# Two attention layers on one core: scores turned round, with queries on partitions and keys along the free axis

## The chip, the core and the metric

The kernel runs on one core of a Trainium2 chip. The core has a matrix engine (TensorE, PE in the profile), a vector engine (VectorE, DVE), an activation engine (ScalarE, ACT), GpSimd (POOL) and a queue engine (SP) that here issues transfers between the device memory and the core's SBUF. Matrix products land in PSUM, in banks of 512 fp32 values on each of 128 partitions. The metric is the device time of one execution in microseconds; lower is better.

## The reference, cut to what matters

Four batch elements (B = 4) with 256 queries of width 512 pass two blocks, each a cross-attention over the same 1601 context rows and a linear layer, with a layernorm in front and the input added behind. All is fp32.

```python
# layer 0: 16 heads; queries and keys of a head are 32 wide, the keys are shared by all heads
C_q, C_kv = Q @ Wq_d, K @ Wkv_d                      # 64 and 32 wide
q = (C_q @ W_qk).reshape(b, n, 16, 32)
attn = softmax(einsum('bnhl,bkl->bhnk', q, C_kv) / sqrt(32))
V = (C_kv @ Wv_u).reshape(b, nkv, 16, 32)
x = x + einsum('bhnk,bkhd->bnhd', attn, V).reshape(b, n, 512)
x = x + layernorm(x) @ dequantize_int4(W0).T + bias
# layer 1: 16 query heads of width 96 on 4 key and value heads; hidden = context and the 256 latents
q, k, v = latents @ Wq.T, hidden @ Wk.T, hidden @ Wv.T     # 1857 keys
x = x + (softmax(q k / sqrt(96)) v) @ Wo.T
H = layernorm(x) @ W1.T + b1
x = x + H + gated low-rank term                       # a few per cent of the work
```

## The kernel before

**Order.** The kernel is written as tasks (`Plan.task`), each with an engine, an estimated duration, its dependencies and the buffers it makes or uses. `Plan.order` runs a list schedule over them with these estimates, nine rounds, and the best round gives the order in which each engine's instructions are written out. On the chip every engine works through its own list in that order; an instruction that waits holds what stands behind it on its engine. `STAGE` and `LINE` fix which heads come next: first the 16 layer 0 heads of batch element 0, then three mixed stages with the 16 layer 1 heads of one element between the 16 layer 0 heads of the next, then the last 16 layer 1 heads. A change of the tensor engine's tile shape is estimated at 0.2 us (`SWITCH`), and a task of another shape is held back a little (`HOLD`).

**A head** (`Head.schedule`). Scores stand with keys on partitions and the 256 queries along the free axis: one 128-key tile gives 128 x 256. In `Head0.score_units` (L1628) and `Head1.score_units` (L1779) four key tiles are computed at a time in four 32-row tiles of the array; a layer 1 head, 96 deep, takes three such steps for each tile, accumulated. Queries are replicated to the four row groups through device memory (`l0_query`, `l0_query_pair`, L787; `l1_query`, L1025 to L1028 and `to_groups`, L362). The score tiles lie in PSUM in two buffers of two banks (`s_psum`). Then, for each head:
- ScalarE copies the scores to SBUF (L1480), four key tiles at a time;
- VectorE takes the maximum over key tiles (L1498, L1501, L1506); TensorE transposes it (L1529), VectorE reduces over the keys that now lie along the free axis (L1533), and TensorE spreads the result back over all partitions (L1542): one maximum for each query;
- VectorE subtracts it (L1554), ScalarE takes the exponential in place (L1563).

**Products.** In layer 1 (`Head1.product_units`, L1804) the stationary operand is a 128-key tile of the values with a column of ones (97 columns), the moving one the 128 x 256 weights: 15 products for each head, and the last row of the result is the softmax's denominator. In layer 0 three tiles and a tile of ones go side by side in column tiles of 32 (`units_of_three`, L1726), with sums on VectorE (`add_up`, L1668, L1671); the first batch element takes two column tiles of 64 (`units_of_two`, L1700). Layer 1 divides after the products (`l1_normalise`), layer 0 in `l0_output`.

**Around the heads.** Keys (`keys`, L923), values (`values`, L863), queries (L1013), output products (`l1_output`, L1161), the linear layers (`linear`, L636) and the latents of the context (`l0_latents`, L663) are full 128 x 128 products over four chunks of the input width, one PSUM bank each (`aux_psum`, two buffers), and are planned into the gaps between heads. The context of one batch element, 3.3 MB, is loaded once into one buffer (`load_ctx`, from ScalarE's queue); keys stay in SBUF in four row groups, values in two halves.

```python
def score_units(self):                                # Head1, before
    def unit(slot, c, step, pss):
        for r in range(4):
            if 4 * slot + r < NK1:
                part = slice(r * 32, (r + 1) * 32)
                nc.tensor.matmul(
                    pss[2 * step + r // 2][:, 2 * (r % 2) + slot % 2, :],
                    lhsT=s["kT", self.kv].tile[part, c, slot, :],
                    rhs=s["q1", self.kv][self.g].tile[part, c, :], ...)
```

Of the kernel before, what the change touches and what calls it, by code (L numbers as in the profile page):

```python
# [14 lines left out]
P = 128  # L15
# [46 lines left out]
class Plan:  # L62
# [11 lines left out]
    def task(self, eng, us, what, deps=(), prio=0.0, new=(), uses=(), lag=0.0, form="full"):  # L74


        t = Task(eng, us, what, [d for d in deps if d is not None], round(prio, 4), new, len(self.tasks))
        t.lag, t.form = lag, form
        for b in (*new, *uses):
            b.users.append(t)  # L80
        self.tasks.append(t)
        return t

    def forward(self, busy):
# [26 lines left out]
        while len(done) < len(self.tasks):  # L111
            best = None
            for eng, tasks in ready.items():
                for t in tasks:
# [6 lines left out]
                    stays = eng != "PE" or t.form == form  # L121
# [12 lines left out]
            t.start = key[0]  # L134
            if t.eng == "PE" and t.form != form:
                t.start += self.SWITCH
            free[t.eng] = t.start + t.us
            if t.eng == "PE":
                form = t.form
            t.end = t.start + t.us + t.lag  # L140
# [15 lines left out]
    def backward(self, done):  # L156
# [13 lines left out]
        for _ in range(len(done)):  # L170
# [8 lines left out]
            free[t.eng] = key[0] + t.us  # L179
# [10 lines left out]
    def order(self, busy):  # L190
        for t in self.tasks:
            for d in t.deps:
                d.next.append(t)
        best = None
        for i in range(self.ROUNDS + 1):
            done = self.forward(busy)
            end = max(t.end for t in done)
            if best is None or end < best[0]:
                best = (end, done)
            self.backward(done)  # L200
        return best[1]
# [3 lines left out]
def xattn_ffn_x2_kernel(  # L205
# [37 lines left out]
    def s_psum(name):  # L243
        return psum.tile([P, 4, T], F32, tag="s", bufs=2, name=name)

    def m_psum(name):
        return psum.tile([P, 2, T], F32, tag="m", bufs=1, name=name)

    def o_psum(name):
        return psum.tile([P, 2, T], F32, tag="o", bufs=1, name=name)  # L250

    def aux_psum(name):
        return psum.tile([P, 512], F32, tag="aux", bufs=2, name=name)
# [4 lines left out]
    DUP = (FULL + 1) * P - S  # L258


# [18 lines left out]
    nc.vector.tensor_scalar(ident, count, number, None, ALU.is_equal)  # L279
    wq_d_sb = const.tile([P, NC, LQ], F32, name="wq_d_sb")  # L280
# [10 lines left out]
    BLOCKS = [(0, 512), (512, 512), (1024, S - 1024)]  # L291

    def load_ctx(b, queue=nc.scalar, between=lambda: None):
        t = big.tile([P, NC, S], F32, tag="ctxT", name=f"ctxT_{b}")
        src = ctxT[b].rearrange("(c p) s -> p c s", p=P)
        for a, w in BLOCKS:
            queue.dma_start(out=t[:, :, a : a + w], in_=src[:, :, a : a + w])
            if a == 0:
                between()
# [3 lines left out]
    KV_ORDER = [3, 0, 1, 2]  # L303
    wvT_sb = const.tile([P, NC, KV * HD], F32, name="wvT_sb")

    def load_wv():
        src = wvT.rearrange("(c p) n -> p c n", p=P)
        nc.sync.dma_start(out=wvT_sb[:, :, :HD], in_=src[:, :, 3 * HD :])
        nc.sync.dma_start(out=wvT_sb[:, :, HD:], in_=src[:, :, : 3 * HD])

    first_ctx = load_ctx(0, nc.sync, load_wv)


    WV = (((0, 64), (32, 96)), ((0, 32, 64), (96,)))
    wv_h = [const.tile([P, H0, 33], F32, name=f"wv_{len(rows)}") for rows, _ in WV]

# [6 lines left out]
    for c in range(NC):  # L323
        src = wkT[c * P : (c + 1) * P, :]
        nc.sync.dma_start(
            out=wk_sb[:, c, :, 0:HD],
            in_=src[:, : 3 * HD].rearrange("p (i d) -> p i d", i=3),
        )
        nc.sync.dma_start(
            out=wk_sb[:, c, :, HD:P],  # L330
            in_=src[:, 3 * HD :].rearrange("p (i d) -> p i d", i=3),
        )
# [10 lines left out]
    ctx_at = [t * P for t in range(FULL)] + [S - P]  # L343
    NK0 = FULL + 1
    NK1 = NK0 + NQ
    VW = HD + 1

    ORDER0 = [[0, 4, 1, 5], [2, 6, 3, 7], [8, 12, 9], [10, 11]]  # L350
    ORDER1 = [[0, 4, 1, 5], [2, 6, 3, 7], [8, 12, 9, 13], [10, 14, 11]]

    G_ORDER = [0, 1, 2, 3]

    rsums = tc.dram_tile([B * KV, G * T], F32, name="rsums")
    q0_rows = [tc.dram_tile([P, 2 * T], F32, name=f"q0_rows_{i}") for i in range(2 * B)]

    q_rows = [tc.dram_tile([32, 3 * T], F32, name=f"q_rows_{i}") for i in range(B * KV * G)]

    def to_groups(dst, far):  # L360
        for r in range(4):
            nc.sync.dma_start(  # L362
                out=dst[32 * r : 32 * r + 32].rearrange("l c t -> l (c t)"), in_=far
            )

# [4 lines left out]
    def late_constants():  # L370
        def values(w, rows, picks):
            def blank():
                nc.gpsimd.memset(w, 0.0)
                for r in picks:
                    nc.gpsimd.memset(w[r : r + 1, :, 32:33], 1.0)

            def load():
                for r in rows:
                    nc.sync.dma_start(
                        out=w[r : r + L0, :, 0:32], in_=wv_u.rearrange("l (h d) -> l h d", d=32)  # L380
                    )

            t = task("POOL", 0.9, blank, [], 0.0)
            return task("SP", 0.45 * len(rows), load, [t], 0.0, lag=2.5)
# [11 lines left out]
        book["wv"] = [values(w, *at) for w, at in zip(wv_h, WV)]  # L396
        t = task("POOL", 0.2, clear, [], 12.0)
        book["limes"] = task("SP", 3.6, experts, [t], 12.0, lag=2.5)

# [12 lines left out]
    def item(name, steps, evictions, deps, prio, uses=(), new=(), form="full"):  # L412
# [3 lines left out]
        ps = Buf("aux", 2)  # L416
        last = None
        for us, what in steps:
# [58 lines left out]
    def layernorm(b, name, tag, prio):  # L477
# [65 lines left out]
        for q in range(NQ):  # L543
# [19 lines left out]
                [(xnT, [P, NC, T])] if first else (),  # L563
            )
# [67 lines left out]
    def linear(b, name, xnT, deps, w, prio):  # L632
        for q in range(NQ):

            def step(ps, c, q=q):
                nc.tensor.matmul(  # L636
# [15 lines left out]
    def l0_latents(b, deps, prio):  # L652

        cT = st8[b]["cT"]
        ckvT, ckv = Buf("ckvT", 1), Buf("ckv", 1)


        def step(ps, s):
            for c in range(NC):
                for r in range(4):  # L660
                    t = 4 * s + r
                    if t < NK0:
                        nc.tensor.matmul(  # L663
                            ps[r * L0 : (r + 1) * L0, s * P : (s + 1) * P],
                            lhsT=wkv_d_sb[:, c, :],
                            rhs=cT.tile[:, c, ctx_at[t] : ctx_at[t] + P],
                            start=(c == 0),
                            stop=(c == NC - 1),
                        )

        def clear():
            ckvT.tile = work.tile([P, 4, P], F32, tag="ckvT", bufs=1, name=f"ckvT_{b}")
            nc.gpsimd.memset(ckvT.tile[:, 3, :], 0.0)

        def keep(ps):
            flat = ckvT.tile.rearrange("p s k -> p (s k)")
            nc.scalar.copy(flat[:, : 3 * P], ps[:, : 3 * P])
            nc.scalar.copy(flat[0:L0, 3 * P :], ps[0:L0, 3 * P :])

        t = task("POOL", 0.2, clear, [], prio, [ckvT])  # L680
        done = item(
            f"ckv_ps_{b}",
            chain(4, 1.0, step),
            [("ACT", 0.75, keep, [ckvT], [t])],
            [*deps, t],
            prio,
            [cT],
            form="32 columns",
        )

        def transpose(ps, s):
            nc.tensor.transpose(ps[:, s * P : (s + 1) * P], ckvT.tile[:, s, :], ident)

        def values(ps):
            nc.scalar.copy(
                ckv.tile[:, :, 0, :], ps[:, : NK0 * L0].rearrange("p (t l) -> p t l", l=L0)
            )

        def mask():
            nc.gpsimd.memset(ckv.tile[0:DUP, FULL, :, :], 0.0)  # L700


        def ones():
            ckv.tile = work.tile([P, NK0, 2, L0], F32, tag="ckv", bufs=1, name=f"ckv_{b}")
            nc.gpsimd.memset(ckv.tile[:, :, 1, :], 1.0)

        t = task("POOL", 0.5, ones, [], prio, [ckv])
        turned = item(
            f"ckv_tp_{b}",
            chain(4, 0.11, transpose),  # L710
            [("ACT", 0.59, values, [ckv], [t])],
            [*done, t],
            prio,
            [ckvT],
        )
        st8[b]["ckvT"], st8[b]["ckv"] = ckvT, ckv
        st8[b]["ckvT_done"] = done
        st8[b]["ckv_done"] = [task("POOL", 0.2, mask, turned, prio, uses=[ckv])]

    def l0_query_latent(b, xnT, deps, prio):  # L720
        cqT = Buf("cqT", 1)

        def step(ps, c):
            nc.tensor.matmul(
# [7 lines left out]
        def keep(ps):  # L732
# [11 lines left out]
            "64 columns",  # L744
        )

    def l0_query(b, half, prio):

        stage, cqT, far = Buf("q0s", 1), st8[b]["cqT"], q0_rows[2 * b + half]

        def step(ps, i):
            quad = 2 * half + i
            nc.tensor.matmul(
                ps[:, i * T : (i + 1) * T],
                lhsT=w_qk_sb[:, quad * P : (quad + 1) * P],
                rhs=cqT.tile,
                start=True,
                stop=True,
            )

        def keep(ps):
            nc.scalar.copy(stage.tile, ps)

        def away():
            nc.sync.dma_start(out=far, in_=stage.tile)

        t = item(
            f"q0_ps_{b}_{half}",
            chain(2, mm(T), step),
# [1327 lines left out]
```

## Time and profile before

| | us |
|---|---|
| median of three timed runs (lowest, highest) | 1906.34 (1903.82, 1907.99) |
| profiled execution, first to last instruction (span) | 1899.4 |
| TensorE busy in it | 1844.9 |
| VectorE busy | 1434.3 |
| ScalarE busy | 1149.0 |
| GpSimd busy | 111.7 |

The profile is of one execution, and gives no time for it but its span; the timed runs lie some 7 us above that. "Busy" adds up the instructions that the profiler recorded, with each instant given to one group of instructions. An fp32 matrix product leaves two records on PE, and a transpose one; PEld are the weight loads, which mostly run under earlier products. A row of the groups names the line, engine, operation, result and operands with their shapes, the count, then busy time and the mean of one, then the idle time of the engine ahead of it and what ended that.

### The profile page before, as it was taken

Reading aid. Unit: us, or ns where it says so; the run is one execution under the profiler, and the core shown is the slowest. Engines: PE = TensorE matmul, PEld = TensorE weight load, DVE = VectorE, ACT = ScalarE, POOL = GpSimd, SP = SyncE. Lnnn points to the kernel's source line nnn. Section 1 sums busy time; section 2 is a strip of 40 time slices with the busy share of each in tenths; the row PEclk is TensorE's granted clock in tenths of the full one; section 3 lists DMA queues with packets and bytes.
Section 4 is the critical chain, followed back from the end, with each engine's and each line's share of the span. In section 5 each row is a group of like instructions: output and inputs, shape, how many; then the busy total and the mean of one; then the engine's idle time right before and its main releaser. Section 6 shows DMA issues by size and latency. Waiting matters only on the chain.

```text
span 1899.4 us, 37000 instructions
## 1 busy us (share of the span) xinstructions
PE 1844.9 (97%) x15223; PEld 1295.7 (68%) x15223; DVE 1434.3 (76%) x2200; ACT 1149.0 (60%) x1695; POOL 111.7 (6%) x185
## 2 busy tenths in 40 slices
PE   6999999999999999999999999999999999999996
PEld 4665787676766777666676677766767667777773
DVE  2998358999998554899999835699999964367773
ACT  2888356677676533767677633566767754365550
POOL 1110100000000110000000101000000010100000
PEclk8999999999999999999999999999999999999998
DMA  7210131311100234121100143222110015111121
GB/s 212 66 42 12 66 83 46 83 49 32 37 18 12 66 103 145 46 65 39 38 24 9 23 107 99 96 65 67 32 32 15 10 45 131 54 40 37 40 71 60
DMA packets 116721, 110.03 MB, mean 58 GB/s; under 512 B 69005, under 2 KB 85353, under 8 KB 116169
## 3 DMA queue, kind: packets, MB, share of 16 engines
q1 hardware_dynamic: 110232, 96.98, 18.4%
q10 hardware_dynamic: 6320, 10.69, 1.7%
q8 instruction: 120, 1.97, 0.4%
q14 instruction: 49, 0.39, 0.1%
HBM read 94.46 MB, written 13.17 MB: 57 GB/s over the span
## 4 chain that ended last, share of the span: by engine, by line
PE 83%; DVE 7%; issue 3%; DMA 3%; ACT 2%; SPq 1%; POOL 0%; DVEq 0%; ACTq 0%; POOLq 0%
PE o L1804 20%; PE s L1779 16%; PE v_ps L863 7%; PE k_ps_c L923 6%; PE s L1628 6%; PE o L1726 5%; PE q_ps L1013 4%; PE wo_ps L1161 4%; PE f L636 3%; DVE mx L1501 3%; PE o L1700 2%; DVE S L1554 2%; PE pm L1529 2%; PE pm L1542 2%; PE vu_ps L804 1%
## 5 line engine op out<-in xcount | busy, mean ns | idle before, releaser
L1480 ACT COPY S<-s 128x1024 f32<-128x1024 f32 (+2 forms) x512 | 448.6, 906 | 332.7 <-PE s L1779 121.6
L1554 DVE TENSOR_TENSOR S<-S,pm 128x1024 f32<-128x1024 f32 (+2 forms) x512 | 528.8, 1082 | 36.5 <-PE pm L1542 34.5
L1501 DVE TENSOR_TENSOR mx<-mx,S 128x512 f32<-128x512 f32 (+1 forms) x704 | 463.7, 659 | 116.9 <-ACT S L1480 92.1
L1563 ACT ACTIVATE S<-S 128x1024 f32<-128x1024 f32 (+2 forms) x512 | 472.3, 950 | 124.4 <-DVE S L1554 118.4
L1804 PE MATMUL o<-S,v 128*97 128x256 f32 x1920 | 461.7, 382 | 3.8 <-ACT S L1563 2.5
L1804 PEld LDWEIGHTS o<-S,v 128*97 128x97 f32 x1920 | 301.6, 164 | 113.7 <-issue 24.7
L1779 PE MATMUL s<-q,kT_k_ps_c 32*128 32x256 f32 x4320 | 275.9, 383 | 0.0
L1779 PEld LDWEIGHTS s<-q,kT_k_ps_c 32*128 32x128 f32 x4320 | 225.0, 185 | 48.8 <-issue 20.8
L863 PE MATMUL v_ps<-wvT_sb,ctxT 128*128 128x192 f32 x832 | 158.9, 334 | 11.8 <-DMA wvT_sb<-in_wvT 11.7
L923 PE MATMUL k_ps_c<-ctxT,wk_sb 128*128 128x384 f32 (+1 forms) x480 | 157.9, 455 | 0.9 <-DVE xnT_xn_tp_a L541 0.9
L863 PEld LDWEIGHTS v_ps<-wvT_sb,ctxT 128*128 128x128 f32 x832 | 136.0, 192 | 32.0 <-issue 16.4
L1628 PE MATMUL s<-q,ckvT 32*128 32x256 f32 x1664 | 150.9, 411 | 5.2 <-DMA q<-q_rows 4.8
L1628 PEld LDWEIGHTS s<-q,ckvT 32*128 32x128 f32 x1664 | 93.5, 185 | 57.0 <-issue 27.0
L1726 PE MATMUL o<-S,ckv 128*32 128x256 f32 x1728 | 127.4, 384 | 0.6 <-DVE S L1671 0.4
L1498 DVE TENSOR_TENSOR mx<-S 128x512 f32<-128x512 f32 x128 | 89.0, 695 | 46.1 <-ACT S L1480 45.5
L923 PEld LDWEIGHTS k_ps_c<-ctxT,wk_sb 128*128 128x128 f32 x480 | 78.7, 189 | 45.4 <-issue 15.5
L1013 PE MATMUL q_ps<-xnT_xn_tp_a,wq 128*128 128x256 f32 x384 | 98.3, 387 | 0.9 <-ACT p_q_ps L1022 0.9
L1533 DVE TENSOR_REDUCE m<-pm 128x2 f32<-128x256 f32 x128 | 53.9, 421 | 56.3 <-PE pm L1529 55.7
L933 ACT COPY kT_k_ps_c<-k_ps_c 32x384 f32<-32x384 f32 (+1 forms) x180 | 76.8, 427 | 32.2 <-PE k_ps_c L923 30.0
L1671 DVE TENSOR_TENSOR S<-S,S 128x512 f32<-128x512 f32 x144 | 88.3, 613 | 9.9 <-ACT S L1480 0.5
L1779 PE MATMUL s<-q,kTlast_k_ps_c 32*128 32x256 f32 x1440 | 93.7, 385 | 0.0
L1161 PE MATMUL wo_ps<-wo,oT 128*128 128x512 f32 x192 | 92.3, 604 | 0.0
(143 smaller groups left out, 1427.8 us busy)
## 6 DMA issues: line engine op xcount, KB each, us to landing
q<-q_rows SPq DMA_DIRECT2D x256, 96.0 KB
wq<-in_wqT SPq DMA_DIRECT2D x48, 192.0 KB
wo<-in_woT SPq DMA_DIRECT2D x16, 576.0 KB
q<-q_rows SPq DMA_DIRECT2D x128, 64.0 KB
ctxT<-in_ctxT ACTq DMA_DIRECT2D x6, 1024.0 KB
q_rows<-p_q_ps SPq DMA_DIRECT2D x48, 96.0 KB
rb<-rsums SPq DMA_DIRECT2D x15, 288.0 KB
ctxT<-in_ctxT ACTq DMA_DIRECT2D x3, 1154.0 KB
```

The lines of the kernel that those rows point to most:

```text
L863: nc.tensor.matmul(ps[:, i * 2 * HD : (i + 1) * 2 * HD], lhsT=src.tile[:, c, tiles[i][1] : tiles[i][1] + P], rhs=wvT_sb[:, c, half * 2 * H ...
L923: nc.tensor.matmul(out, lhsT=wk_sb[:, c, i, :], rhs=rhs, start=(c == 0), stop=(c == NC - 1),)
L1013: nc.tensor.matmul(ps[:, :T], lhsT=wq.tile[:, c, :], rhs=xnT.tile[:, c, :], start=(c == 0), stop=(c == NC - 1),)
L1161: nc.tensor.matmul(ps, lhsT=oT.tile[:, i, q * P : (q + 1) * P], rhs=wo.tile[:, i, :], start=(i == 0), stop=(i == G - 2),)
L1480: nc.scalar.copy(S4[g].tile[:, :n, :], self.scored(ps[g].tile, g))
L1501: nc.vector.tensor_tensor(mx.tile[:, :w, :], mx.tile[:, :w, :], t[:, a : a + w, :], ALU.max)
L1554: nc.vector.tensor_tensor(s[:, :n, :], s[:, :n, :], om.tile[:, 1:2, :].to_broadcast([P, n, T]), ALU.subtract,)
L1563: nc.scalar.activation(s[:, :n, :], s[:, :n, :], AF.Exp, scale=self.scale)
L1628: nc.tensor.matmul(pss[2 * step + r // 2][:, 2 * (r % 2) + s % 2, :], lhsT=st8[self.b]["ckvT"].tile[part, s, :], rhs=qr[part, self.h % 2, ...
L1726: nc.tensor.matmul(po[32 * r : 32 * r + 32, :], lhsT=lhsT, rhs=rhs, start=start, stop=stop)
L1779: nc.tensor.matmul(pss[2 * step + r // 2][:, 2 * (r % 2) + slot % 2, :], lhsT=s["kT", self.kv].tile[part, c, slot, :], rhs=s["q1", self.kv ...
L1804: nc.tensor.matmul(po[:VW, :], lhsT=s["v", j // 2].tile[:, t, j % 2, :], rhs=self.S[g].tile[:, i, :], start=(k == 0), stop=(k == NK1 - 1),)
```

## The change

Scores are turned round: queries on partitions, keys along the free axis. With that the maximum of a query lies within a partition, and the weights have to be turned before the product with the values.

- **Scores.** A unit of layer 1 takes 32 queries of a head as the stationary operand, in each of the four column tiles of the array, and 480 keys as the moving one: column tile c holds the keys whose place in their 128-key tile is 32c to 32c+31. The 96 dimensions are one step. In layer 0 (K = 32) a unit is 16 tiles of 32 x 32: four row groups with four query blocks, into four banks, by four column tiles. Scores lie in a ring of six PSUM banks (`banks`); missing keys are columns filled once with a large negative number.
- **Softmax.** VectorE reduces each bank along the free axis, straight from PSUM. The four column tiles hold four parts of one query's keys, so their maxima meet in a small product (`gather`) with a constant matrix `place`, followed by a small minimum (the sign and the scale are in `place`). ScalarE takes the exponential from PSUM with that as its bias, and sums it (`accum_out`) in the same instruction. VectorE turns the result in 32 x 32 blocks into `Pt`, keys on partitions. The copy to SBUF, the full transposes, the subtraction and the sums of `add_up` are gone. Layer 1 does this for two banks at a time, layer 0 for four.
- **Products.** Four column tiles with the values as the stationary operand: layer 1 packs the 12 blocks of 32 value columns of a group's four heads into three units, layer 0 two heads with two key tiles each. The denominators come from the exponentials' sums.
- **Dense products** go through a helper, `matmul`, that splits the stationary operand into four column tiles of 32; most of the work then has one tile shape. Layernorm's transposes stay full. `aux_psum` has one buffer (`NA = 1`).
- **Transfers.** The replication of the queries is gone. Keys and values pass through device memory (`k_rows`, `v_rows`), where the parts of a group are put together, and come back for each key head (`load_keys`, `load_values`). The context comes in blocks of 384 keys (the last 449) in two buffers, blocks 0 and 1 twice (`SWEEP`), from SP's queue. `STAGE` is a new pattern, "1111" + "0001010101" * 2 + "00101011".

```diff
-    def s_psum(name):
-        return psum.tile([P, 4, T], F32, tag="s", bufs=2, name=name)
+    NB, NA = 6, 1
+    banks = psum.tile([P, NB, 512], F32, tag="s", bufs=1, name="banks")
...
+    def matmul(out, lhsT, rhs, start, stop):
+        for a, w in splits(lhsT.shape[-1], 32):
+            nc.tensor.matmul(
+                out[a : a + w], lhsT=lhsT[:, a : a + w], rhs=rhs, start=start, stop=stop
+            )
...
+            def peaks(j, step):
...
+                nc.vector.tensor_reduce(
+                    mx.tile[:, k : k + step],
+                    banks[:, ps[j].at : ps[j].at + step, self.skip :],
+                    AX.X,
+                    ALU.max,
+                )
...
+            def gather():
+                for c in range(4):
+                    nc.tensor.matmul(
+                        banks[32 * c : 32 * c + 32, ps[blocks[0]].at, : 4 * w],
+                        lhsT=place[:, self.layer, :],
+                        rhs=mx.tile[:, lo:hi],
...
+                nc.scalar.activation(
+                    ex[j // 2].tile[:, j % 2, :n],
+                    banks[:, ps[j].at, self.skip :],
+                    AF.Exp,
+                    bias=mx.tile[:, k : k + 1],
+                    scale=SCALES[self.layer],
+                    accum_out=self.sum_at(4 * m + j),
+                )
...
+                nc.vector.transpose(
+                    self.Pt.tile[:, : n // 32, 32 * j : 32 * j + 64].rearrange(
+                        "p b (j i) -> p j b i", i=32
+                    ),
+                    ex[k].tile[:, :, :n].rearrange("p j (b i) -> p j b i", i=32),
+                )
...
+            def unit():                                     # Head0
+                for r in range(4):
+                    for c in range(4):
+                        n, part = N0 + SHORT[c], slice(32 * r, 32 * r + 32)
+                        nc.tensor.matmul(
+                            banks[32 * c : 32 * c + 32, ps[r].at, self.skip : self.skip + n],
+                            lhsT=s["q0", self.h // 8].tile[part, self.h % 8, 32 * m : 32 * m + 32],
+                            rhs=s["ckvT"].tile[part, c, :n],
...
+            def unit(j):                                    # Head1
+                q = 32 * (4 * m + j)
+                for c in range(4):
+                    n = N1 + SHORT[c]
+                    nc.tensor.matmul(
+                        banks[32 * c : 32 * c + 32, ps[j].at, self.skip : self.skip + n],
+                        lhsT=s["q1", self.kv].tile[:, self.g, q : q + 32],
+                        rhs=s["kT", self.kv].tile[:, c, :n],
...
+            blocks = [divmod(4 * p + j, 3) for j in range(4)]
+
+            def unit(t, po):
+                for j, (h, c) in enumerate(blocks):
+                    nc.tensor.matmul(
+                        po[32 * j : 32 * j + 32, :],
+                        lhsT=v.tile[:, t, 32 * c : 32 * c + 32],
+                        rhs=heads[h].Pt.tile[:, t, :],
...
```

Here N0 is 416 and N1 480, `skip` the rest of a bank's 512 columns, `w` the number of banks treated together, `m` the half of a head's eight blocks of 32 queries.

## The prediction

> **What bounds the kernel now.** I read the page's first two parts, then busy time by stage (cut where the first feed-forward product of each batch element ends), then the groups by line. Engine, busy microseconds, share and instructions:
>
> ```profile
> PE 1844.9 (97%) x15223; PEld 1295.7 (68%) x15223; DVE 1434.3 (76%) x2200; ACT 1149.0 (60%) x1695; POOL 111.7 (6%) x185
> PE   6999999999999999999999999999999999999996
> PEclk8999999999999999999999999999999999999998
> ```
>
> TensorE is the bound from the second slice to the last but one, at full clock. By stage (length, then PE, weight loads, VectorE and ScalarE busy):
>
> ```profile
> 0.00:228.00 228.00, 207.70 (x1463) 136.07 (x1464) 153.99 (x249) 146.78 (x230) 27.53 (x52) 0.98 0.25 72
> 228.00:641.60 413.60, 407.32 (x3619) 284.60 (x3618) 352.09 (x537) 278.34 (x403) 17.53 (x32) 1.00 0.18 49
> 641.60:1099.50 457.90, 452.07 (x3830) 316.72 (x3829) 364.89 (x557) 286.24 (x421) 24.69 (x39) 1.00 0.20 57
> 1099.50:1557.70 458.20, 453.26 (x3840) 318.01 (x3840) 365.05 (x558) 286.85 (x423) 23.98 (x37) 1.00 0.20 57
> 1557.70:1899.40 341.70, 324.52 (x2480) 240.32 (x2478) 198.33 (x301) 150.79 (x218) 18.00 (x25) 0.98 0.23 63
> ```
>
> VectorE stands at 80% in the mixed stages: not much of TensorE's time can go before VectorE is next. Prices of matmuls come from the chain of waits, where runs without a gap stand (start, length, records):
>
> ```profile
> 247.19 2.80 PE s L1779 x48
> 1633.49 9.10 PE v_ps L863 x56
> 1642.59 3.45 PE o L1804 x16
> ```
>
> L1804 takes 0.216 us a record of 256 columns, L863 0.163 us for 192: 0.84 ns a column. Every fp32 product leaves two records, so a matmul of 256 columns costs 0.432 us. L1779, four row tiles at once, takes 2.80 us for 48 records, six units of four: 0.43 us a unit and 0.2 for the start. The timeline shows the same of four column tiles (L1726, 24 records = three units), with the shapes beside it:
>
> ```profile
> 423.16 2.12 PE L863 MATMUL v_ps<-wvT_sb,ctxT 128*128 128x192 f32 x12
> 425.21 1.50 PE L1726 MATMUL o<-S,ckv 128*32 128x256 f32 x24
> 426.64 0.43 PE L1542 MATMUL pm<-ident,m 128*128 128x128 f32 x2
> ```
>
> So four packed tiles cost what one full matmul of the same columns costs, and a change of shape costs extra: 12 x 0.163 us from 423.16 ends at 425.11, the next shape starts at 425.21. Over the trace's 746 changes of shape the wait has a median of 0.094 us, and the first pass, with weights not loaded ahead, is about 0.07 late: 0.165 a change.
>
> With these prices (transposes leave one record, 0.107 us) PE's order gives 190, 395, 440, 440 and 312 us for the stages, changes included: 1776 in all. The stages are 38, 19, 18, 18 and 30 us longer: the start (PE waits 11.7 us for its first weights), short waits, the tail. The sum describes this kernel to within those 123 us; I use it for the new one.
>
> **The change, TensorE.** Counts are from PE's instruction order, whole kernel:
> - Layer 1 scores: 768 units of 256 columns (331.6 us) become 512 of 480 (0.805 each, 412.2): +80.6. Here it loses: 96 of 128 rows are used, before all were.
> - Layer 1 products: 960 of 256 (414.4) become 720 packed units (310.8): -103.6. Twelve 32-wide value blocks of four heads fill three units, and the row of ones goes.
> - Layer 0 scores: 256 units (110.5) become 128 units of 16 tiles and 416 columns (0.698 each, 89.4): -21.1.
> - Layer 0 products: 352 units (151.9) become 224 (96.7): -55.2.
> - Keys, values, output projections of layer 0: -11; the dense products split into four column tiles keep their columns.
> - The transposes around the maximum, 512 records, 55 us, go; 384 gathers of four small matmuls come. Their nearest row is L663, the same packed shape with 128 columns: 3.61 us for 16 units in the chain, 0.23 each, 88 us: +33. Bounds: 0.11 (stream alone) and 0.30 (L1206, 4.8 us for 16 matmuls of 8 columns).
> - Changes of shape: 746 become 341: -67.
>
> Sum -142. By stage the new order needs 162, 375, 407, 406 and 283 us.
>
> **The change, VectorE.** Priced from these groups (count, busy, mean ns):
>
> ```profile
> L1554 DVE TENSOR_TENSOR S<-S,pm 128x1024 f32<-128x1024 f32 (+2 forms) x512 | 528.8, 1082 | 36.5 <-PE pm L1542 34.5
> L1501 DVE TENSOR_TENSOR mx<-mx,S 128x512 f32<-128x512 f32 (+1 forms) x704 | 463.7, 659 | 116.9 <-ACT S L1480 92.1
> L1533 DVE TENSOR_REDUCE m<-pm 128x2 f32<-128x256 f32 x128 | 53.9, 421 | 56.3 <-PE pm L1529 55.7
> L1480 ACT COPY S<-s 128x1024 f32<-128x1024 f32 (+2 forms) x512 | 448.6, 906 | 332.7 <-PE s L1779 121.6
> ```
>
> Subtractions, maxima and sums (some 1300 us) go. In come 512 reductions of 480 and 256 of 832 from PSUM (0.66 and 1.03 us: L1533's 0.421 at 256, with the 1.06 ns a column between L1501's 256 and 512 forms), 602 us; 768 tiny operations (0.19, as L1287 at 32 columns), 146 us; and 512 block transposes of 960 or 832 columns. No row shows these. Below, the cast (0.45 us for 512) gives 0.85; above, the slowest row by column is the reciprocal (1.75 us for 256), 6.5 us. I take the elementwise rows, which also read and write SBUF once: 1.18 and 1.05, 571 us. With the 135 of the rest: about 1450, as before; a mixed stage gets 360 of its 430 us.
>
> The Trainium skill, "VectorE: DVE Perf Modes", section "The three transpose paths", has 311 ns for a 128x128 block transpose in bf16. Scaled in proportion, an estimate, that is 2.3 us for 960 columns, and VectorE would reach 2000 us; with its fixed part paid once it is 1.2. No row here decides.
>
> **ScalarE** loses its copies (448.6 us); the exponentials read PSUM, 0.56 and 0.51 us by L1480's slope, plus a bias and a running sum that no row shows: 0 to 0.26 us more (the shortest copy). 715 to 980 us, off the path except through the banks.
>
> **Queues.** SP loses 384 query loads and 104 query stores, and gets 168 key stores, 60 value stores, 64 reads back and 24 context blocks; it issues 609 transfers, was 772. A store waits on SP for ScalarE's eviction, and the query weights' loads stand behind it; they are two buffers deep, so I set that at nothing (uncovered: the eviction, 0.5 us, for each of 57 a stage, at most 30 us). DMA engines were 18% busy. The key and value round trip takes the place of the query round trip ahead of each layer 1 (4.1 us there); I set it at no cost, covered by the leftover context products; uncovered, 5 us a stage.
>
> **What is new on the path: the first stage.** Layer 0's unit takes four of six PSUM banks, so the next waits for two exponentials of the one before: scores 0.9 with their drain, two reductions 2.1, tiny operation 0.2, gather 0.4, tiny 0.2, two exponentials 1.3, handoffs 0.4: 5.5 to 5.9. Thirty-two of these, 25 us ahead and 12 behind: 225 us, where TensorE needs 162 (plus 12 of start). This stage gains 3, not 28. Elsewhere the gather adds a queue: PE runs its planned order, so a gather that waits for VectorE holds every product behind it; on ScalarE the exponentials wait for the gather's result, and the evictions of the dense products stand behind them. There are 96 in a mixed stage against 64 pairs of transposes, so I raise the 18 us of waits to 25; the tail keeps 30.
>
> Sum: 225 + 400 + 432 + 431 + 313 = 1801 against 1899.4. The median of the timed runs, 1906.3, lies 7 us above the profiled span: about 1808, -5%.
>
> **Rivals.**
> 1. VectorE becomes the bound, through the block transposes. Each mixed stage holds 128 of them; 0.77 us more for one lifts 360 to 458, the stage of before. At twice my price (2.2) the stages are some 250, 475, 500, 500 and 320: about 2050 us, slower. It decides from about 1.85 us a transpose. For it: no row shows the operation, and VectorE has no slack. Against: all elementwise rows lie at 1.06 ns a column.
> 2. The banks: a layer 0 unit in a mixed stage finds its four banks late. 1 us for each of 32 units in three stages is 96 us: about 1900, no change; 2 us, 1990. For it: six banks in a fixed ring, one bank for the dense products (two before), late exponentials. Against: layer 1's work stands between the units.
> 3. The 16 tiles don't run together. Four row tiles (L1628) and four column tiles (L1726) do; both at once no row shows. Four at a time cost 128 x 2.1 us = 268 more: about 2070. The Trainium skill ("TensorE: Matmul & The Clock Gate", Part 3) gives 10.6 times for 16 tiles, not 16; by that the layer 0 scores take 135 us, not 89, an estimate, and the total 1854.
>
> **How the numbers follow.** Forecast, TensorE bound, 1715 to 1880: 0.62 (1715 is gathers at 0.11 and no added waits). Rival 2: 0.13, most of it between 1870 and 1960. Rival 1: 0.15. Rival 3: 0.05. Anything else, split: 0.05. Faster 0.70, same 0.02, slower 0.28; 0.2% is about what a measurement of this kernel tells from no change. The forecast's own range is 1715 to 1880; the range for 8 in 10 goes on to 1985, transposes at 1.9 to 2 us or two late microseconds a unit.
>
> **What would show it.** Right: PE over 90% busy in the mixed stages, packed 480-column units 0.80 us apart, block transposes near 1.1 us, about 340 changes of shape, a first stage near 225 us with PE near 75%. Wrong: VectorE above 95% in the mixed stages (rival 1), PE waiting for exponentials ahead of score lines (rival 2), a 16-tile unit above 1 us (rival 3).

## The result and the profile after

The changed kernel takes 3021.5 us (median of four runs, 3018.8 to 3023.8), the kernel before 1906.3 in the same series (1903.8 to 1908.0): a ratio of 1.586, interval 1.584 to 1.588. Forecast were 1808 us and a range of 1715 to 1985. The time is far outside it, on the other side of no change.

The page of the changed kernel, the same three lines that were shown of before (busy time of each engine; TensorE's busy share in 40 slices, in tenths, and under it the clock that it was granted, in tenths of full speed):

```profile
PE 2166.4 (72%) x27579; PEld 803.8 (27%) x27579; DVE 1367.4 (45%) x2434; ACT 872.1 (29%) x2519; POOL 110.9 (4%) x191
PE   6774767676777878767676778767677687777676
PEclk8996878797786879688787788878877687877778
```

No engine is full. TensorE went from 97% to 72% busy, VectorE stands at 45% and ScalarE at 29%. So no engine has become the bound: they wait for each other. And TensorE's clock, full before, is down in most slices. By stage, cut at the same place as before (length; PE, weight loads, VectorE, ScalarE and GpSimd busy; granted clock; DMA):

```profile
0.00:326.90 326.90, 212.97 (x3336) 88.29 (x3336) 162.20 (x280) 121.75 (x368) 31.27 (x67) 0.83 0.26 70
326.90:1011.50 684.60, 493.76 (x6340) 185.67 (x6341) 325.95 (x571) 213.12 (x620) 18.87 (x38) 0.79 0.14 35
1011.50:1738.40 726.90, 531.05 (x6882) 195.64 (x6878) 339.11 (x595) 217.98 (x629) 24.74 (x43) 0.81 0.15 40
1738.40:2471.50 733.10, 538.64 (x6847) 193.16 (x6843) 336.28 (x584) 208.05 (x597) 20.55 (x29) 0.80 0.13 35
2471.50:3022.00 550.50, 389.99 (x4191) 141.05 (x4183) 203.85 (x404) 111.20 (x305) 15.50 (x14) 0.78 0.13 37
```

The loss is in all stages, and most of it where layer 1 heads run: the mixed stages were to take 400, 432 and 431 us. The list of waits says who waits for whom (total us, times, longest):

```profile
DVE mx L1497 <- PE banks L1759: 444.1, 195, 19.8
PEld banks L1759 <- DVE mx L1497: 402.3, 188, 4.7
PEld banks L1759 <- ACT P L1534: 375.5, 195, 4.0
DVE mx L1497 <- ACT P L1534: 330.8, 179, 6.2
ACT P L1534 <- PE banks L1759: 313.0, 159, 7.9
```

L1759 are layer 1's scores, L1497 the reductions, L1534 the exponentials. Two of these rows can't come from the data. A score unit needs a bank that the exponentials have read; a reduction frees nothing for it, yet the second row has scores waiting for reductions. An exponential gets its bias from VectorE, later than its scores; yet in the last row it waits 313 us for a score unit, which must be one of another bank. The timeline shows how it looks (start, length, instruction, idle time before and what ended it):

```profile
2757.50 1.00 PE L1759 MATMUL banks<-kT,q_q_ps 96*32 96x480 f32 x8 [1.58 <-DVE mx L1497]
2758.58 0.66 DVE L1497 TENSOR_REDUCE mx<-banks 128x1 f32<-128x480 f32 x1 [1.14 <-PE banks L1759]
2759.30 1.00 PE L1759 MATMUL banks<-kT,q_q_ps 96*32 96x480 f32 x8 [0.79 <-DVE mx L1497]
2760.38 0.66 DVE L1497 TENSOR_REDUCE mx<-banks 128x1 f32<-128x480 f32 x1 [0.93 <-PE banks L1759]
...
2768.59 0.66 DVE L1497 TENSOR_REDUCE mx<-banks 128x1 f32<-128x480 f32 x1 [1.99 <-PE banks L1759]
2769.28 0.66 ACT L1534 ACTIVATE P<-banks,mx 128x480 f32<-128x480 f32 x1 [1.89 <-DVE mx L1497]
...
2770.07 0.66 DVE L1497 TENSOR_REDUCE mx<-banks 128x1 f32<-128x480 f32 x1 [0.82 <-ACT P L1534]
```

Score unit, reduction, score unit, reduction: each starts 0.06 to 0.08 us after the one before has ended, though the next unit goes to the next bank. A bank takes 1.80 us (2757.50 to 2759.30). Even a reduction and an exponential, which both only read, take turns (2768.59 to 2770.07).

### The profile page after: what moved, and what is told of

It reads as the page before. It is cut to its first block, busy times and chain, and to the rows that moved or that the text cites. A ratio compares the mean times of both kernels' runs of the same rounds, so it can differ in the third digit from the quotient of the medians.

```text
span 3022.0 us, 62655 instructions
## 1 busy us (share of the span) xinstructions
PE 2166.4 (72%) x27579; PEld 803.8 (27%) x27579; DVE 1367.4 (45%) x2434; ACT 872.1 (29%) x2519; POOL 110.9 (4%) x191
## 5 line engine op out<-in xcount | busy, mean ns | idle before, releaser
L1534 ACT ACTIVATE P<-banks,mx 128x480 f32<-128x480 f32 (+1 forms) x1024 | 642.8, 632 | 1569.6 <-DVE mx L1523 564.2
L1759 PE MATMUL banks<-kT,q_q_ps 96*32 96x480 f32 (+2 forms) x4096 | 700.6, 757 | 458.5 <-DVE mx L1497 234.0
L1497 DVE TENSOR_REDUCE mx<-banks 128x1 f32<-128x480 f32 (+1 forms) x768 | 584.7, 774 | 895.1 <-PE banks L1759 444.1
L1547 DVE STREAM_TRANSPOSE Pt<-P 128x960 f32<-128x960 f32 (+1 forms) x512 | 561.5, 1103 | 240.7 <-ACT P L1534 216.3
L1781 PE MATMUL o<-Pt,v 128*32 128x256 f32 x5760 | 427.0, 426 | 5.5 <-DVE Pt L1547 3.5
L1759 PEld LDWEIGHTS banks<-kT,q_q_ps 96*32 96x32 f32 x4096 | 103.4, 125 | 856.4 <-DVE mx L1497 402.3
L1781 PEld LDWEIGHTS o<-Pt,v 128*32 128x32 f32 x5760 | 211.8, 122 | 166.1 <-issue 90.1
L1534 ACT ACTIVATION_READ_ACCUMULATOR P<-banks,mx 128x1 f32 x1024 | 200.8, 196 | 0.0
L401 PE MATMUL v_ps<-wvT_sb,ctx_b 128*32 128x384 f32 (+1 forms) x1632 | 184.0, 561 | 11.5 <-ACT ks_v_ps L887 6.3
L401 PE MATMUL k_ps_c<-ctx_b,wk_sb 128*32 128x384 f32 (+1 forms) x1536 | 177.0, 580 | 5.3 <-ACT ks_k_ps_c L939 2.3
L1705 PE MATMUL o<-Pt,ckv 128*32 128x256 f32 x1664 | 153.0, 477 | 4.9 <-DVE Pt L1547 4.2
```

The lines of the kernel that those rows point to most:

```text
L401: nc.tensor.matmul(out[a : a + w], lhsT=lhsT[:, a : a + w], rhs=rhs, start=start, stop=stop)
L1497: nc.vector.tensor_reduce(mx.tile[:, k : k + step], banks[:, ps[j].at : ps[j].at + step, self.skip :], AX.X, ALU.max,)
L1534: nc.scalar.activation(ex[j // 2].tile[:, j % 2, :n], banks[:, ps[j].at, self.skip :], AF.Exp, bias=mx.tile[:, k : k + 1], scale=SCALES[se ...
L1547: nc.vector.transpose(self.Pt.tile[:, : n // 32, 32 * j : 32 * j + 64].rearrange("p b (j i) -> p j b i", i=32), ex[k].tile[:, :, :n].rearr ...
L1705: nc.tensor.matmul(po[32 * c : 32 * c + 32, :], lhsT=latents(t), rhs=pair[c // 2].Pt.tile[:, t, :], start=(k == 0), stop=(t + 2 >= NK0),)
L1759: nc.tensor.matmul(banks[32 * c : 32 * c + 32, ps[j].at, self.skip : self.skip + n], lhsT=s["q1", self.kv].tile[:, self.g, q : q + 32], rh ...
```

## The experiments

**Theory A.** `banks` is one PSUM tile of six banks. Accesses of different engines to one tile are put in the order of the program, whichever banks they go to. Scores, reductions, gathers, minima and exponentials all touch this one tile, so the ring of six does not pipeline them. **Theory B.** The chain from score to exponential through six banks is long by itself. **Theory C.** The packed products let the clock fall, and that is the loss.

### The same banks in six, three and two tiles

```diff
-    banks = psum.tile([P, NB, 512], F32, tag="s", bufs=1, name="banks")
+    banks = [psum.tile([P, 512], F32, tag=f"s{i}", bufs=1, name=f"bank{i}") for i in range(NB)]
...
-                            banks[32 * c : 32 * c + 32, ps[j].at, self.skip : self.skip + n],
+                            banks[ps[j].at][32 * c : 32 * c + 32, self.skip : self.skip + n],
```

> The changed kernel with its six score banks as six PSUM tiles of one bank each, in place of one tile of six banks; the planned order, the banks and the sums are the same, only layer 0's reduction over two banks is issued as two of one. Theory A (accesses of different engines to one PSUM tile are put in the order of the program, even where they go to different banks, so scores, reductions and exponentials run one after another): the waits go and the time falls from 3021 us to between 1750 and 2000 us, TensorE is over 90% busy and its mean granted clock is back above 0.95. Theory B (the chain score, reduction, gather, minimum, exponential through six banks is long by itself): 2850 to 3060 us. Theory C (the packed products themselves let the clock fall to 0.80): the clock stays near 0.80 and the time at 2300 us or more.

> The same six banks as three PSUM tiles of two banks each; all instructions are those of the changed kernel. Theory A: part of the false order is left, within pairs of banks, so the time lies between that of one tile (3021 us) and that of six, nearer to six: 1850 to 2400 us. Theories B and C: within 3% of 3021 us.

> The kernel with six tiles, but its six banks as two PSUM tiles of three banks each; order and banks are the same. The false order now holds within three banks. Theory A (order by tile): between the 1918 us of three tiles and the 3021 us of one, 2050 to 2500 us, with a mean granted clock between 0.80 and 0.966. If the loss of the changed kernel came from its one tile in another way than by order within a tile (its address, say), there is no such step and the time is that of three tiles within 2%.

| the six banks lie in | us | TensorE busy | mean granted clock |
|---|---|---|---|
| one tile (the change) | 3021.5 (4 runs) | 72% | 0.80 |
| two tiles of three | 2241.0 (1 run) | 82% | 0.94 |
| three tiles of two | 1918.2 (1 run) | 90% | 0.97 |
| six tiles of one | 1875.5 (4 runs, 1870.6 to 1881.0) | 91% | 0.96 |

Six tiles against the kernel before: 0.984, interval 0.982 to 0.987. The planned order, the banks and the work are the same in all four, but that the kernels with two and six tiles issue layer 0's reduction over two banks as two of one; the kernel with three tiles does not, and stands in the series all the same. What differs is how the banks are grouped into tiles, and the time follows it from step to step. Theory A is shown; B and C, which expected no such series, are out. With six tiles the engines work on different banks at once. Its timeline, in a mixed stage: layer 1 scores run beside layer 0's four reductions, and later beside exponentials.

```profile
1008.62 1.81 PE L1761 MATMUL bank<-kT,q_q_ps 96*32 96x480 f32 x16
...
1008.69 2.08 DVE L1499 TENSOR_REDUCE mx<-bank 128x1 f32<-128x416 f32 x4 [1.11 <-PE bank L1683]
...
1013.04 1.80 PE L1761 MATMUL bank<-kT,q_q_ps 96*32 96x480 f32 x16
...
1013.48 0.60 ACT L1536 ACTIVATE P<-bank,mx 128x416 f32<-128x416 f32 x1
```

In its list of waits the rows "scores after reductions" (402.3 us) and "exponentials after scores" (313.0) are gone; scores still wait for exponentials, which do free banks, 55.1 us where it was 375.5:

```profile
PEld bank L1761 <- ACT P L1536: 55.1, 115, 1.3
```

The Trainium skill, "PSUM — Partial Sum Buffer", section "PSUM bank collisions raise a hardware error", asks for two engines to be kept apart on the same bank and quadrant, and says that different banks run clean. The six-tile trace agrees; the one tile kept them apart over six banks, and that is a matter of the program, not of the memory.

The six-tile kernel is the change without the false order, so its stages are those the prediction priced (first the engines' totals):

```profile
PE 1712.8 (91%) x27579; PEld 824.6 (44%) x27579; DVE 1338.1 (71%) x2700; ACT 832.0 (44%) x2519; POOL 110.9 (6%) x191
0.00:281.90 281.90, 217.03 (x3336) 88.53 (x3336) 165.61 (x354) 118.83 (x368) 31.26 (x67) 0.85 0.30 81
281.90:687.00 405.10, 380.41 (x6336) 185.56 (x6340) 318.89 (x635) 203.38 (x620) 18.94 (x38) 0.98 0.22 60
687.00:1129.40 442.40, 415.14 (x6882) 199.33 (x6878) 332.38 (x659) 207.07 (x629) 24.77 (x43) 0.99 0.23 66
1129.40:1565.10 435.70, 416.11 (x6847) 200.39 (x6843) 326.25 (x648) 197.77 (x597) 20.51 (x29) 0.98 0.21 59
1565.10:1879.20 314.10, 284.08 (x4191) 150.74 (x4183) 194.96 (x404) 105.00 (x305) 15.41 (x14) 0.96 0.22 64
```

282, 405, 442, 436 and 314 us stand against 225, 400, 432, 431 and 313 predicted. Of the 1143 us between the two spans (3022.0 and 1879.2), 454 are longer busy time of TensorE for the same products (2166.4 against 1712.8) and 689 are time in which it is not busy. Some 400 of the 454 are the lower clock, by an estimate: 907 us of the busy time fall where the trace has the clock at half, against 112 with six tiles, and half of that time is lost.

### Is the clock a cause or a consequence?

The next two use one tile of five banks, which leaves a bank free; their order is planned anew for five. The filling stands ahead of each gather and each score unit.

```diff
-    NB, NA = 6, 1
+    FILL, NB, NA = True, 5, 1                 # False in the base
...
+    def fill(n):
+        for _ in range(n if FILL else 0):
+            for c in range(4):
+                nc.tensor.matmul(
+                    spare[32 * c : 32 * c + 32, : NC * LQ],
+                    lhsT=ident[:, 32 * c : 32 * c + 32],
+                    rhs=wq_d_sb.rearrange("p c n -> p (c n)"), start=True, stop=True)
```

> The base for the next run: the changed kernel with one tile of five score banks in place of six (layer 0's reductions over two banks issued as two of one), the eighth bank free. Theory A (the order is that of the tile, so the number of banks in it hardly counts): 3000 to 3150 us at a granted clock of 0.78 to 0.82. Theory B (the ring's depth decides): above 3300 us.

> The same with TensorE kept at work in its waits: two units of four packed tiles with 256 columns go to the eighth bank ahead of each gather and each layer 0 unit, one ahead of each layer 1 unit, and nothing reads them; 1536 units, 664 us of TensorE at full clock, where it waited some 850 us. If TensorE's waits themselves lower its clock: the granted clock rises above 0.90, and the time stays within 5% of the run before this one or falls below it, in spite of the added work. If the clock falls for another reason: it stays near 0.80 and the time rises by 200 us or more.

One run each: 2971.3 us without, 2914.5 with the filling. The pages, without and then with it:

```profile
span 2969.5 us, 62838 instructions
PE 2159.3 (73%) x27579; PEld 798.1 (27%) x27579; DVE 1386.7 (47%) x2690; ACT 862.9 (29%) x2519; POOL 111.0 (4%) x191
PEclk8976878786776889778776788978776677877678
```

```profile
span 2912.7 us, 87414 instructions
PE 2468.9 (85%) x39867; PEld 1193.3 (41%) x39867; DVE 1388.5 (48%) x2690; ACT 864.2 (30%) x2519; POOL 111.2 (4%) x191
PEclk9997999999998999999999999999999999999997
```

TensorE does 12288 more records (1536 units), its clock goes from a mean of 0.78 to 0.96, and the kernel becomes 57 us faster: the waits lower the clock. With the clock back it still takes 2914 us, so the lower clock follows from the waits and adds to the loss. How the 1143 us divide between them stays open, since the filling itself takes time on TensorE's queue. Five banks took no longer than six (2971 against 3021; 3000 to 3150 was expected, so the run lies just outside): in one tile, a bank less in the ring cost nothing.

### What is left of the prediction: ScalarE, the first stage, shapes, gathers

These start from the six-tile kernel, 1875.5 us.

```diff
-                    accum_out=self.sum_at(4 * m + j),      # the sums are set once to 1.0
```

> Six tiles, and the exponentials leave out their running sum (the denominators are a constant, set once by GpSimd), so the 1024 reads of the accumulator, 0.2 us each, go. If the sums lie off the path but for the first stage, where two of them stand in each layer 0 unit (32 x 0.2 to 0.4 us): 1860 to 1873 us against 1875.5. If ScalarE's late exponentials hold the banks in all stages (rival 2 of the prediction), some 200 us of ScalarE go off the path and the time is below 1840 us.

The exponentials leave out their sums here. 1848.3 us (1846.9 to 1852.1), between the two expectations. The stages are 277, 395, 432, 429 and 317: the first gains 5 us, a little less than the 6 to 13 that the chain of a unit would give, and the mixed ones 10, 10 and 7. The accumulator's reads (0.2 us each) thus reach TensorE a little in every mixed stage, in two ways: the weight loads of layer 1's scores wait 30.9 us for exponentials in place of 55.1, and those of the gathers 110.5 us for VectorE in place of 146.7. The first is rival 2's mechanism; both together come to some 10 us a stage, and not the 32 that it began with.

```diff
-        span, step = 4, 2
+        span, step = 2, 2
```

> Six tiles, with layer 0's maxima met for two banks at a time, as layer 1's are, in place of four: 128 more gathers with their two small VectorE operations, but a unit's first two banks come free after two reductions, not four. If the first stage is set by the chain of a unit (6.35 us each now): about 1 us less for each of its 32 units, the first stage at 240 to 260 us against 282. The mixed stages pay 96 more gathers at 0.25 to 0.4 us of TensorE, some 25 to 40 us. Sum 1870 to 1900 us. If the first stage is set by something else, it stays at 275 or more and the time is above 1900 us.

1882.5 us (1880.6 to 1883.8). The first stage falls to 262 us, the next four take 427, 437, 438 and 318: what the shorter chain gives early is lost again later. The added gathers and small operations are there, but the order is planned anew too and moves work between the stages, so what they cost by themselves is not shown. So it is wanted in the first stage alone:

```diff
+            self.span = 2 if b == 0 else 4
```

> Six tiles, with two banks at a time in layer 0 for the first batch element alone (four at a time in the others). If the 20 us that two banks at a time saved in the first stage and the 26 us that they cost in the later ones are separate: the first stage at 262 us, the others as with six tiles (405, 442, 436, 314): 1850 to 1862 us. If the later stages only swap what the first one loses (work for the gaps of the first stage moved to them): 1870 us or more.

1858.5 us (1856.4 to 1861.9), 0.975 of the kernel before (0.974 to 0.977), with stages of 262, 401, 439, 436 and 317: the first stage keeps its gain and the others stay as they were. This version beats both kernels.

```diff
-        for a, w in splits(lhsT.shape[-1], 32):
-            nc.tensor.matmul(
-                out[a : a + w], lhsT=lhsT[:, a : a + w], rhs=rhs, start=start, stop=stop
-            )
+        nc.tensor.matmul(out, lhsT=lhsT, rhs=rhs, start=start, stop=stop)
```

> Six tiles, with the dense products issued whole (the helper no longer splits the stationary operand into four column tiles of 32); the order of the work is the same, so changes of tile shape rise from 341 to 939 in TensorE's order. By the prediction's prices (four packed tiles cost what one full one costs, 0.165 us a change): 598 more changes, 99 us of TensorE's time, less what falls into its waits: 1930 to 1980 us. If a change costs nothing that a packed unit does not cost too: 1865 to 1885 us. If packed tiles cost more than full ones: below 1860 us.

1935.8 us (1931.3 to 1937.4), 60 us more for 598 more changes of shape. TensorE's busy time rises by 82 us (1795.0 against 1712.8): 0.14 us a change, of which 0.10 reaches the end, if a full product costs what four packed ones do. The price of 0.165 was near and somewhat high, and splitting the dense products is what keeps them in one shape.

```diff
...
-            t = task("PE", 0.22, gather, [t], at + AT_TURN, uses=[mx, first], form=COLS)
-            t = task("DVE", 0.1, top, [t], at + AT_SPREAD, uses=[mx, first])
```

> Six tiles, without the gather and the small minimum: each partition takes the maximum of its own quarter of the keys, scaled by a small VectorE operation in the place of the spreading one, so the weights of a query's four quarters have different scales. By the prediction's price (0.23 us for each of 384 gathers, 88 us) 1780 to 1800 us. If the gather costs its stream alone (0.11 us each, 42 us): 1825 to 1840. If the queue ahead of it counts too (TensorE stands 52 us ahead of gathers, waiting for the small product): 1710 to 1750 us.

1850.9 us (1847.6 to 1858.4): only 25 us, less than any of the three expectations. The order is planned anew without these steps, and the stages are 258, 391, 447, 441 and 315: 24 and 14 us less in the first two, 4 and 5 more in the next two. So the 25 us are not the price of the gathers alone. TensorE's busy time falls by 27 us (1685.7 against 1712.8), 0.07 us a gather, and the six-tile timeline shows why it is so little:

```profile
1011.05 0.26 PE L1516 MATMUL bank<-mx,place 128*32 128x16 f32 x6
...
1011.14 0.40 PE L1783 MATMUL o<-Pt,v 128*32 128x256 f32 x1
```

The gather's records last 0.26 us, but the product behind it starts 0.09 us after it. Over 383 gathers the median from a gather's first record to the next product is 0.088 us; 384 of them are 34 us. The prediction took 0.23 us, the spacing of units of 128 columns (L663), for units of 8 or 16 columns; even its lower bound, 0.11, was above what they hold the engine for.

```diff
-            t = task("DVE", 0.1, apart, [t], at + AT_SPREAD, uses=[mx])
-            t = task("PE", 0.22, gather, [t], at + AT_TURN, uses=[mx, first], form=COLS)
-            t = task("DVE", 0.1, top, [t], at + AT_SPREAD, uses=[mx, first])
+            t = task("DVE", 0.18, apart, [t], at + AT_SPREAD, uses=[mx])
+            t = task("PE", 0.3, gather, [t], at + AT_TURN, uses=[mx, first], form=COLS)
+            t = task("DVE", 0.17, top, [t], at + AT_SPREAD, uses=[mx, first])
```

> The kernel before this one in the list (six tiles, two banks at a time for the first batch element), with the three small steps at their measured durations in the plan (0.18, 0.3 and 0.17 us, were 0.1, 0.22 and 0.1): only the order of the instructions moves. If the plan's short estimates put gathers too early, TensorE's 52 us of waits ahead of them fall: 1835 to 1855 us. If not, within 0.7% of the kernel before it either way.

1880.4 us (1875.1 to 1881.6), 1.2% slower than the same kernel with the short estimates: outside both expectations. The order changes as a whole (stages 272, 416, 444, 432, 316). Better estimates of three small steps did not make a better order; why is open.

## Why the prediction was wrong, step by step

**The step that failed** is the sentence that raised the mixed stages' waits from 18 to 25 us, together with rival 2's price. Both took a bank to be free for the next score unit once its own exponential had read it, and counted six of them. That is how the plan counts. It is not how the instructions wait: with one tile the mixed stages' time outside TensorE's busy time is 191, 196 and 194 us, and busy time itself grows by 113 to 123 us a stage over six tiles. The chain of the first stage and the tail's 30 us count the banks in the same way: 327 and 551 us stand there against 225 and 313. Rival 2 named the right row ("PE waiting for exponentials ahead of score lines") and was given 0.13; its mechanism, the late banks of layer 0's units, was too narrow. It explains nothing of scores waiting for reductions, or of layer 1. The sign was at hand in the diff, which replaces two PSUM buffers by one tile; the prediction has no term for it.

**What held**, by the six-tile kernel, in which the failed step is taken out:
- Stages: the mixed ones and the tail within 2.4% (405, 442, 436, 314 for 400, 432, 431, 313). Part of that is luck: two prices of TensorE were too high and the waits too low.
- Score units of layer 1 follow each other at 0.755 us (0.805 predicted), 26 us less over 512. The prediction took 480 columns for all four column tiles; in the trace two of them have 449 and 448. Sixteen tiles run together: 0.898 us to the next unit's start, change of shape included, for 0.698 + 0.165. Rival 3 is out.
- Gathers hold TensorE for 0.088 us, not 0.23. These two make a mixed stage's need some 20 us smaller than predicted; what comes on top of it is then 50 to 55 us, not 25.
- VectorE: the block transposes, which no row of before had, are the elementwise price (1.18 and 1.05 us predicted), and rival 1 is out. So are the reductions (0.66):

```profile
L1549 DVE STREAM_TRANSPOSE Pt<-P 128x960 f32<-128x960 f32 x256 | 294.8, 1164 | 22.8 <-PE o L1783 13.3 <-ACT P L1536 9.3
L1549 DVE STREAM_TRANSPOSE Pt<-P 128x832 f32<-128x832 f32 x256 | 266.6, 1042 | 133.8 <-ACT P L1536 125.9
L1499 DVE TENSOR_REDUCE mx<-bank 128x1 f32<-128x480 f32 x512 | 315.4, 645 | 114.8 <-PE bank L1761 73.7 <-ACT P L1536 36.9 <-issue 0.3
```

  The estimate from the Trainium skill, "VectorE: DVE Perf Modes", section "The three transpose paths", scaled in proportion from 311 ns to 2.3 us, was not what happened; its other reading, 1.2 with the fixed part paid once, was.
- ScalarE: 832 us, within 715 to 980.

**What was mis-sized.** In the list of TensorE's savings the items add up to -144 us, not -142, which is of no account. The first stage takes 282 us with six tiles, 225 predicted. The first unit starts at 37.4 us; I had set 25, though in the kernel before the first scores start at 37.0 too. The 32 units take 6.35 us each (31 steps from 37.4 to 234.1), 5.5 to 5.9 predicted. The trace's clock records split these steps: 19 of them lie wholly at full clock and take 5.73 us on average, as predicted; the other 12, in which the clock is halved for a part or all of the time, take 7.3. So the chain was priced well, and what the prediction left out is the clock: it took full speed throughout, and this stage was granted 0.85. Whether the long steps lower the clock or the low clock makes them long is not shown. A term that the chain doesn't have is in the timeline too: the next unit's reductions stand on VectorE behind the two transposes of the unit before.

```profile
37.44 2.90 PE L1683 MATMUL bank<-ckvT,q_q_ps 32*32 32x416 f32 x32
...
155.66 2.22 DVE L1549 STREAM_TRANSPOSE Pt<-P 128x832 f32<-128x832 f32 x2 [1.41 <-ACT P L1536]
155.67 0.23 PEld L1683 LDWEIGHTS bank<-ckvT,q_q_ps 32*32 32x32 f32 x32 [0.62 <-issue]
...
157.81 2.05 DVE L1499 TENSOR_REDUCE mx<-bank 128x1 f32<-128x416 f32 x4
...
234.14 3.75 PE L1683 MATMUL bank<-ckvT,q_q_ps 32*32 32x416 f32 x32
```

The scores begin at 155.67, the reductions at 157.81. And 48 us follow the last unit's start, where I had 12 behind the last unit's end: the last products, the next element's context and the first linear layer. These 57 us, with 21 in the other stages, are why six tiles give 1875.5 us, -1.6%, and not the -5% that I forecast.

## What to carry to other kernels

Before pricing a ring of PSUM banks, look at what the program makes wait: banks that different engines are to use at the same time belong in tiles of their own, and slices of one tile may be ordered as one. A list of waits in which an instruction waits for work whose data it doesn't use is the sign; group the same memory in another way and see whether the time follows. The length of a record is not the time that it holds its engine: take the distance to the next start.

## What was not expected of the hardware

The clock of TensorE falls with short waits. The Trainium skill, "TensorE: Matmul & The Clock Gate", section "HAM oscillation — how this bites in real kernels", gives as the rule no idle gaps above some 3.4 us. In the changed kernel's trace TensorE has 812 gaps, 316 above 1 us but only seven above 3.4, and its granted clock drops to half 126 times, for 1213 us in all. With six tiles (37 gaps above 1 us, two above 3.4) it drops 20 times, for 146 us. Seven long gaps do not account for 126 drops, so that rule by itself does not cover this trace. Filling the waits with matmuls that nobody reads (an estimated 664 us of them at full clock) raised the clock enough to shorten the kernel by 57 us.
